# Tile 0's product in halves ahead of the leftovers, weights added on GpSimd; layer 1's direct sums scaled in pieces

## The chip, the cores and the metric

One core of one Trainium2 chip. The metric is the device time of one execution in microseconds (us). In what follows a run is one execution; each kernel was run several times, in rounds that alternate with the kernel before on the same chip. "The span" is the time from the first to the last instruction of the one execution that was traced; the run's time is about 1.7 us longer. In the profile lines PE is TensorE, PEld its weight loads, DVE VectorE, ACT ScalarE, POOL GpSimd and SP SyncE; L347 is line 347 of that run's kernel, and the numbers shift a little from kernel to kernel. A "hole" is a stretch in which TensorE is idle, a product's "lead" the time by which it is ready before TensorE wants it.

## The reference, cut to what matters

Two layers of a compressed interaction network on `x` of 4096 rows, 32 fields, 16 columns. Each layer multiplies every pair of fields elementwise, mixes the products with a weight matrix, and normalizes over the whole batch. Half of layer 1's outputs ("direct") go straight to the result, the other half feed layer 2.

```python
def _cin_layer(out, x, W, b, gamma, beta):
    h = jnp.einsum('rne,rfe->rnfe', out, x).reshape(r, -1, e)
    h = jnp.einsum('rce,oc->roe', h, W) + b[None, :, None]
    return _batchnorm(h, gamma, beta)            # mean and variance over rows and columns
h1 = _cin_layer(x, x, W1, b1, g1, beta1)         # 32x32 pairs -> 128
out, direct1 = (h1[:, :64], h1[:, 64:])
direct2 = _cin_layer(out, x, W2, b2, g2, beta2)  # 64x32 pairs -> 128
return jnp.concatenate([direct1, direct2], axis=1).sum(axis=-1)
```

## The kernel before

Layer 1 works through 128 tiles of 512 sites (a site is one row and column). As the pairs (i, j) and (j, i) have the same product, their weights are added (`w1 += w1m`) and only half of the products are made: per tile a "main" product of 128x2048 on VectorE, and per eight tiles one "leftovers" product of 128x512 for the 16 pairs (i, i+16). TensorE takes four main matmuls a tile, each 128x512, and per four tiles four small leftovers matmuls that open four accumulators. Each of these matmuls stands in the traces as two passes (1024 for the 512 main matmuls), so a tile's main matmuls are x8. The order in the code at the start is the leftovers' product, the main product, the leftovers' matmuls, the main matmuls; in the traces VectorE makes tile 0's main product first, then adds the weights, then makes the leftovers' product:

```python
BEGIN = 6                                        # warm-up matmuls on ones, ahead of everything
...
        nc.vector.tensor_tensor(w1_sb, w1_sb, w1m_sb, ALU.add)
...
        for t in range(NT):
            s = t % GROUP                        # GROUP = 8
            if s == 0:
                zr = rpool.tile([P, T], FP, tag="zr", name="zr")
                nc.vector.tensor_tensor(zr, r[:, :T], r[:, T:], ALU.mult)
            ...                                  # loads of tile t+1
            product = nc.vector.tensor_tensor(z, a..., b..., ALU.mult)     # 128x2048
            if s % 4 == 0:
                for k in range(4):
                    ps = pss[t + k] = psum.tile([P, T], FP, tag="ps", name="ps")
                    rows = slice(32 * k, 32 * (k + 1))
                    nc.tensor.matmul(ps, w1_sb[rows, 4 + s // 4, :], zr[rows, :], start=True, stop=False)
            for m in range(4):
                nc.tensor.matmul(pss[t], w1_sb[:, m, :], z[:, m // 2, m % 2, :], start=False, stop=(m == 3))
            if t > 0:
                finish(t - 1)                    # evict, statistics, sum of the direct half
            if t == 20:
                combine_weights()                # sums of layer 2's weights, six VectorE instructions
            with tc.issue_after(loads[-1].ins), tc.issue_after(product.ins):
                if t == 6:
                    nc.sync.dma_start(w2_sb, w2)
                for first, load in EARLY:        # layer 2's first loads, at t = 12 ... 112
                    if t == first:
                        early.append(load())
```

Layer 2 takes its 64 pairs of tiles in a Strassen-like scheme: ScalarE makes a factor into PSUM, VectorE multiplies it with loaded data (L456 and L461 of before), GpSimd sums these products (L502, L505), TensorE multiplies both kinds (L486). In the first pair of it the direct sums of layer 1 are finished and written:

```python
            if c == 0 and k == 1:
                with tc.issue_after(lasts["dve"].ins), tc.issue_after(lasts["act"].ins):
                    write_direct()     # a reduction, four tiny factors, one 128x2048 scaling, two writes on ScalarE's queue
```

## Time and profile before

| what | kernel before | read from |
|---|---|---|
| time | 2128.49 us, median of 3 (2127.01 to 2129.0) | the runs |
| span | 2125.7 us | the trace |
| TensorE busy | 2094.9 us | busy shares |
| leftovers' first matmul | 12.09 us | timeline |
| last statistics of layer 1 begin | 493.90 us | timeline of VectorE |
| from there to the end | 1631.8 us | 2125.7 less 493.90 |

The last two rows cut the program in two: whatever part 1 of the change does must show in the first number, whatever part 2 does in the second. One line marks the cut:

```profile
493.90 0.70 DVE L106 BATCH_NORM_STATS2 stats<-ps 128x6 f32<-128x512 f32 x1 [2.02 <-PE ps L357]
```

### The profile page before, as it was taken

How to read it: one execution, taken by the hardware profiler on the slowest of the kernel's cores; microseconds unless marked ns; L12 is line 12 of the kernel's file. 1: busy time of each engine (PE TensorE's matmuls, PEld its weight loads, DVE VectorE, ACT ScalarE, POOL GpSimd, SP SyncE). 2: the span in 40 equal slices, each digit the busy share in tenths (PEclk: the TensorE clock that was granted, in tenths of full speed). 3: DMA queues.
4: the chain of work that ended last, by engine and by line, in shares of the span. 5: the costliest groups of instructions: out<-in, count | busy, mean ns of one | idle time of the engine just before them, and what ended most of it. 6: DMA issues, size and time to landing. Idle time of an engine off the chain costs nothing.

```text
span 2125.7 us, 23431 instructions
## 1 busy us (share of the span) xinstructions
PE 2094.9 (99%) x8732; PEld 736.7 (35%) x8732; DVE 1912.0 (90%) x1461; ACT 855.6 (40%) x1233; POOL 1328.7 (63%) x390
## 2 busy tenths in 40 slices
PE   9999999999999999999999999999999999999996
PEld 3444444443333333333333333333333333333332
DVE  7988889887999999899999998999999989999996
ACT  3555555554333333333333333333333333433332
POOL 0000000003888888878888888788888888888885
PEclk9999999999999999999999999999999999999998
DMA  9999999998667777776768777776677777766751
GB/s 353 360 331 349 326 360 350 362 334 220 161 168 170 178 185 172 172 173 160 164 163 198 173 171 174 173 163 166 162 178 171 170 175 173 163 165 162 171 137 40
DMA packets 112019, 440.65 MB, mean 207 GB/s; under 512 B 13088, under 2 KB 13088, under 8 KB 103456
## 3 DMA queue, kind: packets, MB, share of 16 engines
q1 hardware_dynamic: 105296, 417.38, 73.4%
q10 hardware_dynamic: 6608, 21.77, 2.7%
q8 instruction: 68, 1.11, 0.2%
q14 instruction: 47, 0.39, 0.1%
HBM read 417.07 MB, written 22.02 MB: 207 GB/s over the span
## 4 chain that ended last, share of the span: by engine, by line
PE 85%; POOL 9%; DVE 3%; issue 2%; ACT 1%; DMA 0%; DVEq 0%; SPq 0%; POOLq 0%
PE x L486 62%; PE ps L357 21%; POOL t L505 5%; POOL t L502 3%; PE ps L355 2%; DVE zz L456 2%; ACT both L448 1%; DVE e L451 0%; DMA b<-in_xb 0%; DVE zz L461 0%; PE running L375 0%; DVE x L188 0%; DVE d L647 0%; ACT u L448 0%; DVE groupsx L124 0%
## 5 line engine op out<-in xcount | busy, mean ns | idle before, releaser
L486 PE MATMUL x<-zz,w_sb 128*64 128x512 f32 x2560 | 966.1, 592 | 0.0
L486 PE MATMUL x<-zz,s_sb 128*64 128x512 f32 x2048 | 932.4, 592 | 0.7 <-PE running L375 0.7
L502 POOL TENSOR_TENSOR t<-zz 128x1024 f32<-128x1024 f32 x192 | 456.9, 2380 | 760.4 <-DVE zz L456 760.4
L505 POOL TENSOR_TENSOR t<-zz,t 128x2048 f32<-128x2048 f32 x192 | 876.2, 4564 | 15.1
L486 PE MATMUL x<-t,s_sb 128*64 128x512 f32 x1536 | 696.2, 594 | 6.7 <-POOL t L505 6.7
L448 ACT ACTIVATE f<-a,keep 128x512 f32<-128x512 f32 x512 | 398.2, 778 | 632.7 <-DVE zz L456 626.7
L456 DVE TENSOR_TENSOR zz<-f,b 128x2048 f32<-128x2048 f32 x255 | 580.2, 2275 | 1.2 <-ACT f L448 1.2
L456 DVE TENSOR_TENSOR zz<-f,bx 128x2048 f32<-128x2048 f32 x255 | 580.2, 2275 | 0.0
L357 PE MATMUL ps<-z,w_sb 128*128 128x512 f32 x1024 | 449.2, 597 | 0.0
L486 PEld LDWEIGHTS x<-zz,s_sb 128*64 128x64 f32 x2048 | 280.5, 137 | 366.1 <-issue 350.3
L486 PEld LDWEIGHTS x<-t,s_sb 128*64 128x64 f32 x1536 | 205.3, 137 | 456.4 <-issue 397.3
L486 PE MATMUL x<-t,w_sb 128*64 128x512 f32 x768 | 363.1, 595 | 0.0
L345 DVE TENSOR_TENSOR z<-a,b 128x2048 f32<-128x2048 f32 x128 | 293.0, 2289 | 62.7 <-DMA b<-in_xb 33.3
L486 PEld LDWEIGHTS x<-zz,w_sb 128*64 128x64 f32 x2560 | 300.7, 137 | 109.6 <-issue 105.3
L357 PEld LDWEIGHTS ps<-z,w_sb 128*128 128x128 f32 x1024 | 192.4, 190 | 255.0 <-issue 244.7
L486 PE MATMUL x<-zz,neg_sb 128*64 128x512 f32 x512 | 240.6, 592 | 0.0
L307 ACT ACTIVATE e<-ps,bn_sb 128x512 f32<-128x512 f32 x127 | 87.3, 687 | 241.1 <-PE ps L357 235.7
L451 DVE TENSOR_TENSOR both<-both,x 128x512 f32<-128x512 f32 x64 | 44.0, 687 | 129.0 <-ACT both L448 129.0
L448 ACT ACTIVATE u<-e,bn_sb 64x512 f32<-64x512 f32 x64 | 46.2, 722 | 192.9 <-DVE e L451 192.9
L486 PEld LDWEIGHTS x<-zz,neg_sb 128*64 128x64 f32 x512 | 70.1, 137 | 145.9 <-issue 145.9
L486 PEld LDWEIGHTS x<-t,w_sb 128*64 128x64 f32 x768 | 100.1, 137 | 0.0
L448 ACT ACTIVATE both<-x 64x512 f32<-64x512 f32 x64 | 38.0, 593 | 137.5 <-PE x L486 137.5
(74 smaller groups left out, 892.3 us busy)
## 6 DMA issues: line engine op xcount, KB each, us to landing
a<-h SPq DMA_DIRECT2D x256, 512.0 KB, 5.4
a<-in_xa SPq DMA_DIRECT2D x128, 512.0 KB, 6.0
b<-in_xb SPq DMA_DIRECT2D x128, 512.0 KB, 7.0
b<-in_xb SPq DMA_DIRECT2D x64, 1024.0 KB, 7.2
bx<-in_xb SPq DMA_DIRECT2D x64, 512.0 KB, 6.2
bx<-x SPq DMA_DIRECT2D x64, 512.0 KB, 7.9
h<-kept ACTq DMA_DIRECT2D x64, 256.0 KB, 5.9
r<-in_xr SPq DMA_DIRECT2D x16, 512.0 KB, 8.0
```

The lines of the kernel that those rows point to most:

```text
L307: nc.scalar.activation(e, ps, AF.Identity, bias=b1)
L345: product = nc.vector.tensor_tensor(z, a.rearrange("p (a t) -> p a t", a=2).unsqueeze(2).to_broadcast([P, 2, 2, T]), b.rearrange("p (b t) ...
L355: nc.tensor.matmul(ps, w1_sb[rows, 4 + s // 4, :], zr[rows, :], start=True, stop=False)
L357: nc.tensor.matmul(pss[t], w1_sb[:, m, :], z[:, m // 2, m % 2, :], start=False, stop=(m == 3))
L448: return queue("act", lambda: nc.scalar.activation(to, source, AF.Identity, **scale_bias))
L451: return dve(lambda: nc.vector.tensor_tensor(to, x, y, ALU.add))
L456: dve(lambda: nc.vector.tensor_tensor(z, a, b.rearrange("p (k q) t -> p k q t", k=2), ALU.mult))
L486: queue("pe", lambda: nc.tensor.matmul(self.of[x], w, b, start=start, stop=stop))
L502: queue("pool", lambda: nc.gpsimd.tensor_tensor(t2, t3, b11, ALU.add))
L505: queue("pool", lambda: nc.gpsimd.tensor_tensor(t[:, 1:3], z[:, 2:4], twice, ALU.subtract))
```

## The change

Its intent is to let TensorE begin earlier, and to take work out of the first pair of layer 2. Part 1: tile 0's product is made in two halves, its main matmuls go first and the leftovers come behind; the weights are added on GpSimd; two reductions (`spread`, `block`) move from the start to tiles 12 and 14. Part 2: the direct sums' reduction moves to the second pair of layer 2, their factors to the third, the scaling is cut into four pieces over the pairs after it, and the writes go out in the ninth pair on SyncE's queue.

```diff
-    nc.vector.tensor_reduce(spread, select..., AX.X, ALU.max)      # and block
-        nc.vector.tensor_tensor(w1_sb, w1_sb, w1m_sb, ALU.add)
+        nc.gpsimd.tensor_tensor(w1_sb, w1_sb, w1m_sb, ALU.add)
...
-            if s == 0:
-                zr = ...                                            # leftovers first
+            if s == 0 and t > 0:
+                zr = leftovers(r)
+            for k in (slice(0, 1), slice(1, 2)) if t == 0 else (slice(0, 2),):
+                product = multiply_main(z, *main[0], k)
+            if t == 0:
+                with tc.issue_after(product.ins):
+                    zr = leftovers(r)
...
+            if s % 4 == 0 and t > 0:
+                add_leftovers(t, zr)
             for m in range(4):
-                nc.tensor.matmul(pss[t], ..., start=False, stop=(m == 3))
+                nc.tensor.matmul(pss[t], ..., start=(t == m == 0), stop=(t > 0 and m == 3))
+            if t == 0:
+                add_leftovers(t, zr)
...
+                if t == 12:
+                    nc.vector.tensor_reduce(spread, ...)
+                if t == 14:
+                    nc.vector.tensor_reduce(block, ...)
...
-    idle, swaps = [], []
+    idle, swaps = [lambda: sum_direct(NC - 1)], []
...
-            if c == 0 and k == 1:
-                with tc.issue_after(lasts["dve"].ins), tc.issue_after(lasts["act"].ins):
+            if c == k == 2:
+                queue("act", direct_factors)
+            if 3 <= c < 7 and k == 2:
+                queue("act", lambda: scale_direct(c - 3))           # 128x512 each
+            if c == 8 and k == 2:
+                with tc.issue_after(loads[-1].ins):
                     write_direct()                                  # now on nc.sync
```

More of the change, by code (lines that the diff above doesn't have):

```diff
@@ L230, in tile_cin @@
     spread = const.tile([KEEP, P], FP, tag="spread", name="spread")
-    nc.vector.tensor_reduce(spread, select.rearrange("k i n f -> k (n f) i"), AX.X, ALU.max)
     block = const.tile([KEEP, 4], FP, tag="block", name="block")
-    nc.vector.tensor_reduce(block, select.rearrange("k i n f -> k i (n f)"), AX.X, ALU.max)
     hs = [dram.tile([KEEP, 2 * T], FP, tag=f"h{c}", name=f"h{c}") for c in range(NC)]
@@ L324, in sum_direct @@
         def sum_direct(c):
-            nc.vector.tensor_reduce(
+            return nc.vector.tensor_reduce(
                 d1[:, c * RT : (c + 1) * RT],
@@ L330, in sum_direct, with leftovers, add_leftovers, multiply_main @@
             )
+        def leftovers(r):
+            zr = rpool.tile([P, T], FP, tag="zr", name="zr")
+            nc.vector.tensor_tensor(zr, r[:, :T], r[:, T:], ALU.mult)
+            return zr
+        def add_leftovers(t, zr):
+            for k in range(4):
+                rows = slice(32 * k, 32 * (k + 1))
+                ended = t == k == 0
+                nc.tensor.matmul(
+                    pss[t + k], w1_sb[rows, 4 + t % GROUP // 4, :], zr[rows, :], start=not ended, stop=ended
+                )
+        def multiply_main(z, a, b, k):
+            n = k.stop - k.start
+            return nc.vector.tensor_tensor(
+                z[:, k],
+                a.rearrange("p (a t) -> p a t", a=2)[:, k].unsqueeze(2).to_broadcast([P, n, 2, T]),
+                b.rearrange("p (b t) -> p b t", b=2).unsqueeze(1).to_broadcast([P, n, 2, T]),
+                ALU.mult,
+            )
         main = [load_main(0)]
@@ L335, in tile_cin @@
             s = t % GROUP
-            if s == 0:
-                zr = rpool.tile([P, T], FP, tag="zr", name="zr")
-                nc.vector.tensor_tensor(zr, r[:, :T], r[:, T:], ALU.mult)
             if s == 4 and t + 4 < NT:
@@ L342, in tile_cin @@
                 main.append(load_main(t + 1))
-            a, b = main.pop(0)
+            if s == 0 and t > 0:
+                zr = leftovers(r)
             z = zpool.tile([P, 2, 2, T], FP, tag="z", name="z")
-            product = nc.vector.tensor_tensor(
-                z,
-                a.rearrange("p (a t) -> p a t", a=2).unsqueeze(2).to_broadcast([P, 2, 2, T]),
-                b.rearrange("p (b t) -> p b t", b=2).unsqueeze(1).to_broadcast([P, 2, 2, T]),
-                ALU.mult,
-            )
+            for k in (slice(0, 1), slice(1, 2)) if t == 0 else (slice(0, 2),):
+                product = multiply_main(z, *main[0], k)
+            main.pop(0)
+            if t == 0:
+                with tc.issue_after(product.ins):
+                    zr = leftovers(r)
             if s % 4 == 0:
                 for k in range(4):
-                    ps = pss[t + k] = psum.tile([P, T], FP, tag="ps", name="ps")
-                    rows = slice(32 * k, 32 * (k + 1))
-                    nc.tensor.matmul(ps, w1_sb[rows, 4 + s // 4, :], zr[rows, :], start=True, stop=False)
+                    pss[t + k] = psum.tile([P, T], FP, tag="ps", name="ps")
+            if s % 4 == 0 and t > 0:
+                add_leftovers(t, zr)
             for m in range(4):
-                nc.tensor.matmul(pss[t], w1_sb[:, m, :], z[:, m // 2, m % 2, :], start=False, stop=(m == 3))
+                nc.tensor.matmul(
+                    pss[t], w1_sb[:, m, :], z[:, m // 2, m % 2, :], start=(t == m == 0), stop=(t > 0 and m == 3)
+                )
+            if t == 0:
+                add_leftovers(t, zr)
             if t > 0:
@@ L362, in tile_cin @@
             with tc.issue_after(loads[-1].ins), tc.issue_after(product.ins):
+                if t == 12:
+                    nc.vector.tensor_reduce(spread, select.rearrange("k i n f -> k (n f) i"), AX.X, ALU.max)
+                if t == 14:
+                    nc.vector.tensor_reduce(block, select.rearrange("k i n f -> k i (n f)"), AX.X, ALU.max)
                 if t == 6:
@@ L397, in tile_cin, with direct_factors @@
         evict_direct(eds[NC - 1][high, :], last)
-    def write_direct():
-        sum_direct(NC - 1)
-        direct = const.tile([P, 2], FP, tag="direct", name="direct")
+    direct = const.tile([P, 2], FP, tag="direct", name="direct")
+    def direct_factors():
         for half in range(2):
@@ L404, in write_direct, with scale_direct @@
                 to = direct[half * KEEP : (half + 1) * KEEP, k : k + 1]
-                nc.scalar.activation(to, ss1[high, k : k + 1], AF.Identity, scale=factor)
-        nc.scalar.activation(d1, d1, AF.Identity, scale=direct[:, 0:1], bias=direct[:, 1:2])
+                last = nc.scalar.activation(to, ss1[high, k : k + 1], AF.Identity, scale=factor)
+        return last
+    def scale_direct(part):
+        d = d1[:, part * T : (part + 1) * T]
+        return nc.scalar.activation(d, d, AF.Identity, scale=direct[:, 0:1], bias=direct[:, 1:2])
+    def write_direct():
         for half in range(2):
-            nc.scalar.dma_start(
+            nc.sync.dma_start(
                 out[:KEEP, half * (ROWS // 2) : (half + 1) * (ROWS // 2)],
```

## The prediction

> **What bounds the kernel now.** I read the page's busy shares first, then who waited for whom on TensorE, then the timeline of the start and of the opening of layer 2.
>
> ```profile
> PE 2094.9 (99%) x8732; PEld 736.7 (35%) x8732; DVE 1912.0 (90%) x1461; ACT 855.6 (40%) x1233; POOL 1328.7 (63%) x390
> ...
> PE x L486 <- POOL t L505: 6.7, 13, 2.4
> PE ps L355 <- DVE zr L338: 3.0, 1, 3.0
> PE begun L215 <- DVE ones L212: 1.6, 1, 1.6
> PE x L486 <- PE running L375: 0.7, 1, 0.7
> ```
>
> TensorE is busy for 2094.9 of 2125.7 us, and the change removes no matmul. Only TensorE's holes can be won, and they are listed: about 20 us behind its last matmul (untouched here), 3.0 us before the first leftovers (L355), 6.7 us in layer 2 behind GpSimd. There is no wait at all between 12 and 493.7 us.
>
> The start, in the timeline (start, duration, engine, line, what; in brackets the idle time before it):
>
> ```profile
> 8.27 2.29 DVE L345 TENSOR_TENSOR z<-a,b 128x2048 f32<-128x2048 f32 x1 [6.51 <-DMA b<-in_xb]
> 10.48 0.95 DVE L273 TENSOR_TENSOR w_sb<-w_sb,w1m_sb 128x768 f32<-128x768 f32 x1
> 11.35 0.68 DVE L338 TENSOR_TENSOR zr<-r 128x512 f32<-128x512 f32 x1
> 12.09 1.64 PE L355 MATMUL ps<-zr,w_sb 32*128 32x512 f32 x8 [3.04 <-DVE zr L338]
> ...
> 13.48 2.27 DVE L345 TENSOR_TENSOR z<-a,b 128x2048 f32<-128x2048 f32 x1
> ```
>
> Data of tile 0 is there at 8.2 us, then VectorE works three things off in a row before TensorE may begin: the whole product, the weights, the leftovers' product. The warm-up matmuls ended at 9.05 (12.09 less 3.04). The stretches by window show a second cost (columns: window, its length, busy time of PE, PEld, DVE, ACT, POOL, then the granted clock, DMA share, GB/s):
>
> ```profile
> 12.00:14.00 2.00, 1.91 (x9) 0.66 (x10) 2.00 (x4) 0.00 (x0) 0.00 (x0) 0.65 1.07 416
> 14.00:16.00 2.00, 2.00 (x3) 0.82 (x3) 1.94 (x3) 0.00 (x0) 0.00 (x0) 0.50 0.94 328
> 16.00:18.00 2.00, 2.00 (x6) 0.84 (x5) 2.00 (x1) 0.00 (x0) 0.00 (x0) 1.00 0.64 225
> ```
>
> After the hole the clock is halved until 16 us. The price is in the chain of waits, first group against second:
>
> ```profile
> 12.09 1.64 PE ps L355 x8
> 13.72 15.09 PE ps L357 x32
> 28.81 1.07 PE ps L355 x8
> 29.88 13.93 PE ps L357 x32
> ```
>
> The first eight leftover passes and 32 main passes last 16.72 us, start to start; the second set 15.00. So 1.72 us are lost to the clock.
>
> **What the Trainium skill says.** "TensorE: Matmul & The Clock Gate", Part 1: the half-rate state returns after an idle window of about 3.4 us, windows run freely, and full rate takes another such window of work. The trace agrees: idle 9.05 to 12.09, half rate from about 12.6 to 16.0. "VectorE: DVE Perf Modes", section on the TRN2 errata, gives (N+151)/0.96 ns for an fp32 tensor_tensor; the trace has 2.29 us for 2048 and, at L461, 1.21 to 1.23 us for 1024 elements. "GPSIMD Engine Reference", section 3.1, has an add of 2048 at 4497 ns, 1.96 times VectorE's; the trace has 4.57 us. "DMA: Bandwidth & Descriptors", "Issuing engines are not separate DMA queues": another issuing engine saves only issue time; before, ScalarE's queue spends 2.34 us issuing the two output writes.
>
> **The change part by part.**
>
> Part 1, the start. Tile 0's product becomes two products of 1024. The first starts at 8.27 as before and ends 1.23 later, at 9.50 (L461's duration); TensorE follows VectorE by 0.06 (12.03 to 12.09), so it starts at 9.56. The weights must be added by then. On GpSimd, 1024 elements take 2.38 us and 2048 take 4.57, so 768 interpolate to 1.83; the second weight load was issued at 1.32 and landed 5.1 us later, at 6.4; the add ends near 8.3. It is hidden, by 1.2 us. The order of instructions of the new kernel confirms that the first main matmuls wait for VectorE and GpSimd and stand ahead of the leftovers. The second half is done at about 10.6, before the first half's two matmuls (1.72 us of passes) end at 11.3. Leftovers: r landed at 9.5 (2.18+7.3), their product lies at 10.6 to 11.3 and is needed at 13.0. The hole falls from 3.04 to about 0.5 us, far below a window, so the clock should stay up. Won: 12.09-9.56 = 2.53, plus 1.72 of clock, 4.25 us in all.
>
> What takes some back at once: tile 1. Its b was issued at 3.40 and took 8.6 us: 12.0. In the kernel before VectorE came to it only at 13.48, so this was hidden. Now: 12.0+2.3 = 14.3 against TensorE ready at 9.56+3.43+1.07 = 14.06. Cost 0.3; 3.95 us are left.
>
> Then tiles 4 to 16. TensorE moves 3.95 us forward, the products less: loads of tile t+3 go out when product t ends, and those move by 13.48-12.0 = about 1.45. Between 16 and 22 us the DMA share is 0.64 to 0.87, so that fits in; from 22 us on it is 0.99 and more, so it cannot be much more. The products' lead over TensorE before was 4.3 us at tile 4 (ends 25.47, wanted 29.81), 3.6 at tile 8 (41.28 for 44.88), 2.8 at tile 11 (52.39 for 55.2), 3.3 at tile 14 (63.48 for 66.75) and 2.7 at tile 15 (67.47 for 70.2). It shrinks by 2.5: enough everywhere, though only 0.2 to 0.3 at tiles 11 and 15. But the two reductions taken from the start (1.02 and 0.67) come back here: the order of instructions puts one between products 12 and 13 and one between 14 and 15. The first falls into the 2.0 us that VectorE waited for b ahead of product 14. The second, some 0.6, makes product 15 about 0.5 late. Later the lead recovers: product 118 waits for b until 450.81 and still ends 3.7 us before it is wanted, and 50 products wait for TensorE, so the loads keep up. Cost about 0.5; 3.4 us are left.
>
> Part 2, the direct sums. Removed from the first pair of layer 2: a reduction of 0.67 on VectorE, four small and one 2.10 us activation, and 2.34 us of DMA issue on ScalarE, which made VectorE wait 1.18 us at 513.87. But TensorE's holes there come from GpSimd:
>
> ```profile
> 507.83 2.38 POOL L502 TENSOR_TENSOR t<-zz 128x1024 f32<-128x1024 f32 x1 [505.35 <-DVE zz L456]
> 510.29 4.53 POOL L505 TENSOR_TENSOR t<-zz,t 128x2048 f32<-128x2048 f32 x1
> 514.77 2.37 POOL L502 TENSOR_TENSOR t<-zz 128x1024 f32<-128x1024 f32 x1
> 517.23 4.56 POOL L505 TENSOR_TENSOR t<-zz,t 128x2048 f32<-128x2048 f32 x1
> 521.74 2.38 POOL L502 TENSOR_TENSOR t<-zz 128x1024 f32<-128x1024 f32 x1
> 524.19 4.54 POOL L505 TENSOR_TENSOR t<-zz,t 128x2048 f32<-128x2048 f32 x1
> ```
>
> GpSimd runs without a gap from 507.83, and starts after products that precede the removed work. The three holes behind it (2.36, 0.74, 0.72) stay: worth 0. The added work: the reduction now lies in the second pair, 0.6 us ahead of that pair's GpSimd work; GpSimd's last piece ended at 552.78 and was wanted at about 553.74, so 0.36 is left of 0.96. Four activations of about 0.7 (one eviction of 512 columns was 0.68) fall into ScalarE's gaps of 2.54 between factors. The writes move to SyncE's queue in the ninth pair, where the DMA share is about 0.70. Cost 0.
>
> Sum: 4.25-0.3-0.5 = 3.4 us; 2128.5-3.4 = 2125.1 us.
>
> **The rivals.** First, late products: if loads do not move forward at all after tile 3, tiles 4 to 15 lose another 1 to 1.4 us and the gain is about 2: 2126.4. For it: the DMA share of 0.99 from 22 us. Against it: the slack before, and the long-run lead. Second, the clock falls anyway, because windows run freely or the hole is longer than I think (GpSimd late, first loads late): a cold start costs 1.7, leaving about 1.7, 2126.8. Against it: a hole of 0.5 is a seventh of a window. Third, part 2 pays: the freed VectorE time of 1.85 us shortens the opening of layer 2, by at most the 3.8 us of its three holes: 2122 to 2124. Against it: GpSimd's unbroken run. Fourth, part 2 costs: layer 2 runs with hardly any spare time per pair (ten further waits for GpSimd of about 0.3 each exist already), so an activation or a write in the way of a factor may add 0.3 in each of seven pairs, 2 us: 2127.
>
> **Range and chances.** The runs before spread over 2 us, so the median is good to about 0.8. The start is worth 3 to 4 us with some certainty, the give-back 0 to 1.5, part 2 plus or minus 1. Predicted 2125.1 us, 8 in 10 between 2123.2 and 2127.0. A change of 2% would be 42 us, more than all the holes together: faster 0.003, within 2% 0.994, slower 0.003.
>
> **What would show it.** Right: first main matmul near 9.6 us, no half clock after it, tile 1 waiting about 0.3 us for its product; sub-microsecond waits for products at tiles 11 to 15; the end of layer 1 near 490.4 instead of 493.86; first piece on GpSimd 3.4 us earlier as well, and the same three holes behind it. Wrong: half clock after 9.6 us, a wait for GpSimd's weights, TensorE waiting in layer 1 for more than 1.5 us in sum, or a distance from the end of layer 1 to the end that differs by over 0.5 us from before.

## The result, and the profile after

The changed kernel took 2124.68 us (median of 4, 2124.06 to 2127.26) against 2128.3 (median of 4, 2127.01 to 2129.0) for the kernel before in the same rounds. The ratio is 0.9986, 95% interval 0.9969 to 1.0003: the same at 2%, and 3.6 us less by the medians. This interval still reaches past 1; those of after_again and start_only below do not. A ratio here is, to within 0.0001, the mean time of one kernel's runs over that of the other's of the same rounds, so it is not quite the ratio of the two medians. The predicted 2125.1 us lies 0.4 us off.

But the trace taken beside this result did not look like the prediction. It fell on the slowest of the four runs, 2127.26 us (span 2125.5). Its timeline of the start (start, duration, engine, line, what; idle time before it in brackets):

```profile
8.18 1.80 POOL L271 TENSOR_TENSOR w_sb<-w_sb,w1m_sb 128x768 f32<-128x768 f32 x1 [5.70 <-DMA w1m_sb<-in_w1m]
9.10 3.09 DVE L347 TENSOR_TENSOR z<-a,b 128x1024 f32<-128x1024 f32 x2 [7.34 <-DMA b<-in_xb]
11.21 5.37 PE L378 MATMUL ps<-z,w_sb 128*128 128x512 f32 x8 [2.23 <-DVE z L347]
16.50 1.14 PE L340 MATMUL ps<-zr,w_sb 32*128 32x512 f32 x8
```

and its stretches (the granted clock is the third number from the end):

```profile
12.00:14.00 2.00, 2.00 (x4) 0.86 (x3) 1.94 (x4) 0.00 (x0) 0.00 (x0) 0.61 0.98 381
14.00:16.00 2.00, 2.00 (x4) 0.67 (x2) 1.72 (x2) 0.00 (x0) 0.00 (x0) 0.53 0.98 373
```

Four things are off at once: the second weight load landed at 8.03 us instead of the 6.38 that the kernel before had, tile 0's data at 9.1 instead of 8.27, the two halves took 3.09 us rather than the 2.36 of two products of 1.23 us that overlap a little (after_third), and after a hole of 2.23 us the clock was halved all the same, so eight passes took 5.29 us, start to start. The last statistics of layer 1 then began at 493.71, hardly earlier than before. Is this how the changed kernel runs, or one unlucky execution? The first experiment asks that.

### The profile page after: what moved, and what is told of

Same layout as the page of the kernel before. It is cut to its first block, busy times and chain, and to the rows that moved or that the text cites. A ratio compares the mean times of both kernels' runs of the same rounds, so it can differ in the third digit from the quotient of the medians.

```text
span 2125.5 us, 23438 instructions
## 1 busy us (share of the span) xinstructions
PE 2095.5 (99%) x8732; PEld 736.3 (35%) x8732; DVE 1911.2 (90%) x1461; ACT 856.5 (40%) x1236; POOL 1330.4 (63%) x391
## 4 chain that ended last, share of the span: by engine, by line
PE 85%; POOL 9%; DVE 3%; issue 2%; ACT 1%; DMA 0%; DVEq 0%; SPq 0%; POOLq 0%
PE x L521 62%; PE ps L378 21%; POOL t L540 6%; POOL t L537 3%; PE ps L340 2%; DVE zz L491 2%; ACT both L483 1%; DMA b<-in_xb 0%; DVE e L486 0%; DVE zz L496 0%; PE running L404 0%; DVE x L188 0%; DVE z L347 0%; DVE d L687 0%; ACT u L483 0%
## 5 line engine op out<-in xcount | busy, mean ns | idle before, releaser
L347 DVE TENSOR_TENSOR z<-a,b 128x2048 f32<-128x2048 f32 (+1 forms) x129 | 293.6, 2277 | 62.8 <-DMA b<-in_xb 35.9
```

Source lines behind the costliest of these rows:

```text
L347: return nc.vector.tensor_tensor(z[:, k], a.rearrange("p (a t) -> p a t", a=2)[:, k].unsqueeze(2).to_broadcast([P, n, 2, T]), b.rearrange( ...
```

## The experiments

Twelve runs were made, in four sessions, each session on one chip. All outputs are right. Theory A is that of the prediction: the gain is the earlier start of TensorE and the clock that stays up; part 2 is worth nothing. Rivals: part 2 brings the gain (B); the clock alone does (C); and for what is lost on the way, GpSimd's addition or the moved reductions are to blame (D, E). The table holds the results; the readings follow.

| label | edit | median (range) of its runs | before, same rounds | ratio [95%] | first main matmul | last statistics of layer 1 | rest |
|---|---|---|---|---|---|---|---|
| after_again | none | 2124.74 (2123.97 to 2127.33) | 2129.12 | 0.9985 [0.9972, 0.9997] | 9.90 | 490.69 | 1631.9 |
| start_only | part 1 alone | 2124.65 (2124.01 to 2125.48) | 2129.12 | 0.9983 [0.9970, 0.9995] | 9.82 | 491.00 | 1631.9 |
| direct_only | part 2 alone | 2128.06 (2125.58 to 2130.38) | 2129.12 | 0.9997 [0.9985, 1.0010] | (leftovers 11.71) | 492.62 | 1631.9 |
| warm_before | before, three more warm-ups | 2127.66 (2127.42 to 2130.57) | 2129.12 | 1.0000 [0.9987, 1.0014] | (leftovers 12.54) | 493.94 | 1631.8 |
| gpsimd_beside | GpSimd work added | 2138.16 (one run) | 2128.89 | none | 9.88 | 504.16 | 1632.2 |
| dve_weights | weights on VectorE again | 2126.10 (2125.37 to 2127.30) | 2128.89 | 0.9987 [0.9975, 1.0000] | 9.27 | 492.56 | 1632.0 |
| late_reduce | reductions at tiles 60, 62 | 2124.78 (2124.05 to 2125.87) | 2128.89 | 0.9981 [0.9968, 0.9993] | 9.73 | 490.52 | 1632.6 |
| combined | both of these, one more warm-up | 2125.70 (2123.99 to 2128.87) | 2128.89 | 0.9986 [0.9972, 0.9999] | 9.46 | 491.74 | 1632.3 |
| after_third | none | 2124.72 (2124.09 to 2126.30) | 2127.47 | 0.9990 [0.9976, 1.0003] | 9.76 | 490.61 | 1631.7 |
| relaxed | late_reduce, layer 2's weights and loads spread | 2124.70 (2124.25 to 2124.97) | 2127.47 | 0.9987 [0.9975, 1.0000] | 9.97 | 490.79 | 1632.1 |
| relaxed_dve | combined, spread likewise | 2124.24 (2123.34 to 2126.76) | 2127.47 | 0.9987 [0.9975, 1.0000] | 10.43 | 493.15 | 1631.9 |
| before_again | kernel before, none | 2128.21 (2126.47 to 2132.77) | 2128.86 | 1.0006 [0.9993, 1.0020] | (leftovers 12.04) | 492.69 | 1632.0 |

Times in us. "Rest" is the span less the column ahead of it. Each timed kernel had five runs; the kernel before had nine in each of the four sessions, and five more as the control before_again, 41 in all.

### after_again: the changed kernel once more

No edit.

> The changed kernel unchanged, for a second trace, since the first trace fell on a run of 2127.26 us while the three others took 2124.1 to 2125.0. Theory (the start pays): an ordinary run is 3.5 to 4.2 us faster than before, b of tile 0 lands near 8.2 us, the first main matmul begins near 9.6 us, no half clock follows, and TensorE leaves layer 1 near 490.5 us. Rival (the start is always late and the gain comes from layer 2): the trace shows the start at 11 us and the half clock again, and layer 2 shorter by 2 us or more.

The median came back (2124.74), and the trace, now on a run of 2124.36 us, shows what the prediction had drawn:

```profile
6.87 1.80 POOL L271 TENSOR_TENSOR w_sb<-w_sb,w1m_sb 128x768 f32<-128x768 f32 x1 [4.39 <-DMA w1m_sb<-in_w1m]
8.29 2.60 DVE L347 TENSOR_TENSOR z<-a,b 128x1024 f32<-128x1024 f32 x2 [6.53 <-DMA b<-in_xb]
9.90 3.67 PE L378 MATMUL ps<-z,w_sb 128*128 128x512 f32 x8 [1.25 <-DVE z L347]
12.45 2.29 DVE L347 TENSOR_TENSOR z<-a,b 128x2048 f32<-128x2048 f32 x1 [0.78 <-DMA b<-in_xb]
13.50 1.14 PE L340 MATMUL ps<-zr,w_sb 32*128 32x512 f32 x8
14.80 6.71 PE L378 MATMUL ps<-z,w_sb 128*128 128x512 f32 x15 [0.16 <-DVE z L347]
```

```profile
12.00:14.00 2.00, 2.00 (x8) 0.69 (x10) 1.55 (x1) 0.00 (x0) 0.00 (x0) 1.00 1.05 420
14.00:16.00 2.00, 1.84 (x11) 0.68 (x4) 1.65 (x2) 1.33 (x3) 0.00 (x0) 1.00 0.98 381
```

The second fence has the stretches of the same trace. The hole is 1.25 us, the clock stays at 1.00, and the eight passes take 3.60 us where they took 5.29. TensorE waits once for tile 1's product, as foretold, and the last statistics of layer 1 begin at 490.69. So the first trace was one unlucky execution; but the spread between executions is itself part of the story, and after_third below was run to see it again.

### start_only and direct_only: which part brings it

start_only keeps the second half of the code as it was before; direct_only keeps the first half:

```diff
# start_only, against the changed kernel: part 2 undone
-    idle, swaps = [lambda: sum_direct(NC - 1)], []
+    idle, swaps = [], []
-            if c == k == 2: ... / if 3 <= c < 7 and k == 2: ... / if c == 8 and k == 2: ...
+            if c == 0 and k == 1:
+                write_direct()
# direct_only, against the kernel before: only these lines of the change
```

> Part 1 alone: tile 0 in halves, leftovers behind, weights added on GpSimd, the two reductions moved; the direct sums as before. Theory: all of the gain, 3.4 to 4.2 us below before. Rival (part 2 pays too): 1 to 2.5 us below before.

> Part 2 alone: the direct sums in pieces, the start as before. Theory: 0 within 0.4 us, the three waits of TensorE for GpSimd in the first pair stay at 2.4, 0.7 and 0.7 us. Rival (the freed VectorE and ScalarE time opens layer 2 sooner): 1 to 3 us faster.

start_only has all of the gain (ratio 0.9983), direct_only none (0.9997). The interval of direct_only would still allow 3 us, so the traces have to decide: its time after layer 1 is 1631.9 us, where the kernel before has 1631.8. B falls. Where the time of part 2 went shows in two views. The waits between 498 and 530 us, before the change and with part 2 alone:

```profile
PE x L486 <- POOL t L505: 3.8, 3, 2.4
```

```profile
PE x L492 <- POOL t L511: 3.8, 3, 2.4
```

Same sum, same number of waits, same longest one. And in the changed kernel's trace (after_again), GpSimd begins at 504.71 and works without a gap, while VectorE, rid of its reduction and of its wait for ScalarE, merely waits longer for TensorE's sums (5.20 us; in the kernel before it was 3.26):

```profile
504.71 2.37 POOL L537 TENSOR_TENSOR t<-zz 128x1024 f32<-128x1024 f32 x1 [496.04 <-DVE zz L491]
507.16 4.54 POOL L540 TENSOR_TENSOR t<-zz,t 128x2048 f32<-128x2048 f32 x1
511.65 2.39 POOL L537 TENSOR_TENSOR t<-zz 128x1024 f32<-128x1024 f32 x1
...
522.88 0.69 DVE L486 TENSOR_TENSOR both<-both,x 128x512 f32<-128x512 f32 x1 [5.20 <-ACT both L483]
```

The freed time became idle time of an engine that is not the bound there. Taking work off it could not help.

### warm_before: the clock alone

```diff
-BEGIN = 6
+BEGIN = 9
```

> The kernel before with nine warm-up matmuls in place of six, so that TensorE has work until about 11.6 us and the hole ahead of the first leftovers falls from 3.0 to about 0.5 us, with the first leftovers still at about 12.1. It tells the cost of the clock apart from the late start. Theory (the half clock costs 1.7 us of the start): 1.7 us faster, no half clock in the trace, first group of 40 passes 15.0 us long. Rival (the hole costs only its own length): no faster.

Three more warm-up matmuls keep TensorE busy until 12.60 us, 0.4 us past the leftovers' product, so the clock stayed up, and the second group of matmuls began at 27.54 instead of 28.74. Yet the ratio is 1.0000 (the median 1.5 us lower, the interval 3 us wide to either side), and the last statistics of layer 1 begin at 493.94. The 1.2 us were given back at two places: a wait of 0.34 us for the product at tile 7 and one of 0.29 at tile 15, and the two groups around them, leftovers included, took 15.60 and 15.64 us instead of 15.00. This was the first sign that in layer 1 the loads lead TensorE by little: whoever arrives earlier waits later. So in this trace a clock that stayed up won nothing. C alone does not explain the gain, though the interval here is too wide to settle the clock's worth; before_again below does.

### gpsimd_beside: does GpSimd's addition slow VectorE?

In the first trace the halves took 3.09 us. The Trainium skill, "SBUF — State Buffer", section "Who interferes with whom", says that a VectorE instruction with two inputs in SBUF contends with a GpSimd instruction that reads SBUF, not with one that only writes it. The experiment puts both beside layer 1's products (VectorE also sets the scratch tile to ones, once, at the start):

```diff
+            with tc.issue_after(product.ins):
+                if 28 <= t < 36:
+                    nc.gpsimd.tensor_tensor(scratch, w2_sb[...], w2_sb[...], ALU.mult)   # 128x1024, reads SBUF
+                if 44 <= t < 52:
+                    nc.gpsimd.memset(scratch, 1.0)                                       # only writes
```

> The changed kernel with eight GpSimd multiplications of 128x1024 (read and write on-chip memory) and then eight GpSimd memsets of 128x1024 (write only) put beside the products of layer 1, behind the landing of layer 2's weights near 36 us; the result is not changed. In the traces of the changed kernel the first half product took 1.55 and 1.96 us instead of 1.21 where the weights' addition on GpSimd still ran. Theory (a VectorE product with two on-chip operands stands still while a GpSimd instruction that reads runs, or the other way): beside the multiplications either products last 2.3 to 2.4 us longer than 2.29 or GpSimd's 2.38 us grow by as much; beside the memsets the products stay at 2.29. Rival (the first half was long for another reason, such as the loads landing): products stay at 2.29 throughout.

(The expectation's 1.55 us is a misreading: the first half product took 1.46 us in after_again, 1.64 in start_only and 1.96 in the first trace.) The eight multiplications all ran early, in one row from 33.8 us, and the memsets behind them:

```profile
33.77 26.45 POOL L391 TENSOR_TENSOR scratch<-w_sb 128x1024 f32<-128x1024 f32 x8 [25.25 <-DMA w_sb<-in_w]
39.36 4.43 DVE L347 TENSOR_TENSOR z<-a,b 128x2048 f32<-128x2048 f32 x1
50.84 4.43 DVE L347 TENSOR_TENSOR z<-a,b 128x2048 f32<-128x2048 f32 x1
...
60.29 8.02 POOL L398 MEMSET scratch<- 128x1024 f32 x8
60.43 2.28 DVE L347 TENSOR_TENSOR z<-a,b 128x2048 f32<-128x2048 f32 x1
63.24 2.27 DVE L347 TENSOR_TENSOR z<-a,b 128x2048 f32<-128x2048 f32 x1
```

The kernel's products take 2.29 us where GpSimd rests. A product beside a memset takes the same 2.28, one beside a multiplication of GpSimd up to 4.43, and GpSimd's own instructions take 3.31 us on average (26.45 by 8) where layer 2's additions of the same size take 2.38. (Those run beside products as well, but these have one input in PSUM, and they keep their 2.28 us.) The page is right in this case, in both directions. The kernel as a whole took 13 us longer than the changed kernel, nearly all of it in layer 1 (its last statistics begin at 504.16 us instead of 490.69).

With that, the start can be read exactly. In each trace with the addition on GpSimd:

| trace | addition ends | first half begins | they overlap by | first half lasts |
|---|---|---|---|---|
| relaxed (below) | 8.42 | 8.60 | none | 1.23 |
| late_reduce | 8.35 | 8.35 | 0.00 | 1.23 |
| gpsimd_beside | 8.52 | 8.51 | 0.01 | 1.23 |
| after_third | 8.53 | 8.38 | 0.15 | 1.23 |
| after_again | 8.67 | 8.29 | 0.38 | 1.46 |
| start_only | 8.59 | 8.03 | 0.56 | 1.64 |
| first trace | 9.98 | 9.10 | 0.88 | 1.96 |

From 0.15 us of overlap on, the half is longer by just the overlap less 0.15, and it ends 1.08 us after GpSimd in the last three cases: it stands still until GpSimd is done. D holds, though only for executions in which the second weight load is late against tile 0's data.

### dve_weights, late_reduce, combined: undo the two suspects

```diff
# dve_weights
-        nc.gpsimd.tensor_tensor(w1_sb, w1_sb, w1m_sb, ALU.add)
+        weights1 = nc.vector.tensor_tensor(w1_sb, w1_sb, w1m_sb, ALU.add)    # ahead of the first half
# late_reduce
-                if t == 12:    ...spread...     -                if t == 14:    ...block...
+                if t == 60:    ...spread...     +                if t == 62:    ...block...
# combined: both, and
-BEGIN = 6
+BEGIN = 7
```

> The changed kernel with the weights added on VectorE again, but ahead of tile 0's first half product, while VectorE waits for b. Theory (the addition on GpSimd costs the first half product 0.3 to 0.7 us): first half product 1.2 us, 0.3 us faster than the changed kernel in the trace's end of layer 1, more where loads land late; 3.6 to 4.5 us below before. Rival (the addition on VectorE costs as much, since the second weight load lands only shortly before b): same as the changed kernel.

> The changed kernel with the two reductions for layer 2 moved from tiles 12 and 14 to tiles 60 and 62, where the products' lead over TensorE has grown again. Theory (they make product 15 late): no time lost by TensorE in tiles 12 to 15, 0.2 to 0.4 us faster than the changed kernel at the end of layer 1. Rival (the loads of those tiles set it): the loss of 0.2 to 0.4 us in tiles 12 to 15 stays.

> Weights on VectorE ahead of the first half product, the two reductions at tiles 60 and 62, and seven warm-up matmuls in place of six, so that the hole ahead of the first main matmul is nearly closed also where loads land late. Theory: no half clock, 0.4 to 0.8 us faster than the changed kernel, 4 to 5 us below before, with a smaller spread from run to run. Rival: as fast as the changed kernel, because what is won at the start is lost at tiles 9 to 16 to late products, as in the run with warm-up matmuls alone.

dve_weights does what it was made for. The addition takes 0.96 us on VectorE and fits ahead of tile 0's data; the halves take 2.36, and TensorE begins 1.28 us after the first half does (after_again: 1.61):

```profile
6.72 0.96 DVE L271 TENSOR_TENSOR w_sb<-w_sb,w1m_sb 128x768 f32<-128x768 f32 x1 [4.95 <-DMA w1m_sb<-in_w1m]
7.99 2.36 DVE L347 TENSOR_TENSOR z<-a,b 128x1024 f32<-128x1024 f32 x2 [0.31 <-DMA b<-in_xb]
9.27 3.70 PE L379 MATMUL ps<-z,w_sb 128*128 128x512 f32 x8 [0.77 <-DVE z L347]
...
14.58 1.98 PE L379 MATMUL ps<-z,w_sb 128*128 128x512 f32 x4 [0.54 <-DVE z L347]
```

And it is no faster for it: 2126.10 us. It lost 0.54 us at tile 1 at once, and a further 0.77 at tiles 12 to 15, 0.55 between 281 and 296 us, 1.01 between 311 and 327. late_reduce still loses 0.34 us at tiles 12 to 15, though there is no reduction any more: product 15 ends at 66.68 us, against 66.85 and 66.70 in after_again and after_third. So E falls. combined loses 1.49 us in 310 to 326 us, where the first pair's data of layer 2 are being loaded (1 MB at tile 80) on top of layer 1's own loads:

```profile
311.19 7.13 PE L379 MATMUL ps<-z,w_sb 128*128 128x512 f32 x16
318.76 3.70 PE L379 MATMUL ps<-z,w_sb 128*128 128x512 f32 x8 [0.43 <-DVE z L347]
322.98 3.70 PE L379 MATMUL ps<-z,w_sb 128*128 128x512 f32 x8 [0.53 <-DVE z L347]
```

A new theory, F, follows: layer 1 has pinch points, at the places where layer 2's weights and first data are loaded beside layer 1's, and a lead that TensorE gains at the start is partly eaten there.

### after_third, relaxed, relaxed_dve: is it those loads?

after_third is the changed kernel a third time. relaxed is late_reduce with the pinch points spread out; relaxed_dve is combined with the same spreading:

```diff
-                if t == 6:
+                if t == 24:
                     nc.sync.dma_start(w2_sb, w2)
-            if t == 20:
-                combine_weights()
+            if t in range(44, 56, 2):
+                with tc.issue_after(product.ins):
+                    combine_weights((t - 44) // 2)               # one of its six instructions each
-    EARLY += [(72, lambda: load_b(0)), (80, lambda: load_bx(0))]
+    EARLY += [(72, lambda: load_b(0)), (80, lambda: load_bx(0)), (84, lambda: load_bx_rest(0, early[-1]))]
```

> The changed kernel once more, as the measure for the two runs beside it on the same chip: 2124.1 to 2125.3 us in most runs.

> The changed kernel with what loads VectorE and the load queue in layer 1 spread out: layer 2's weights loaded at tile 24 in place of 6 and combined one piece at a time at tiles 44 to 54, the two reductions at tiles 60 and 62, the second half of the first bx load at tile 84 in place of 80. Theory (between tile 2 and the end of layer 1 TensorE loses time only where extra loads or extra VectorE work meet a thin lead): no loss after tile 1 in the trace, end of layer 1 at about 490.3 us, 0.2 to 0.4 us faster than the changed kernel. Rival (the loads of layer 1 by themselves are too slow for a TensorE that started earlier): losses of the same size at tiles 4 to 16 or later.

> The same spreading, with the weights on VectorE ahead of the first half product and seven warm-up matmuls, as in the combined kernel. Theory: what the combined kernel lost at tiles 80 to 84 (1.5 us in its trace) is gone, end of layer 1 at about 490.0 us, 1 to 1.5 us faster than the combined kernel, 4.5 to 5 us below before, the fastest of all. Rival: as slow as the combined kernel, 3 us below before.

At the first pinch point F holds. The same group of 32 passes (tiles 12 to 15) in late_reduce and in relaxed, where 14.00 us is the time without a wait:

```profile
56.10 14.33 PE L378 MATMUL ps<-z,w_sb 128*128 128x512 f32 x32
```

```profile
56.71 14.00 PE L383 MATMUL ps<-z,w_sb 128*128 128x512 f32 x32
```

TensorE comes 0.61 us later here, and that alone would have covered the 0.34. But VectorE also makes product 15 1.34 us earlier, again late_reduce and then relaxed:

```profile
64.40 2.28 DVE L347 TENSOR_TENSOR z<-a,b 128x2048 f32<-128x2048 f32 x1
```

```profile
63.06 2.28 DVE L352 TENSOR_TENSOR z<-a,b 128x2048 f32<-128x2048 f32 x1
```

Its lead is 1.76 us, where in late_reduce it was 0.06. So the spreading did it, not the later start; which of its pieces did, was not separated.

relaxed does not wait anywhere in layer 1 after tile 1. But its first data came late (TensorE began at 9.97), so it arrives at the end of layer 1 with all the others, at 490.79. Its median, 2124.70, is that of the changed kernel; its five runs lie within 0.7 us, which may be chance. In relaxed_dve the losses only moved on, to 326 to 388 us, beside the further loads of layer 2 that begin at tile 88:

```profile
380.97 7.13 PE L384 MATMUL ps<-z,w_sb 128*128 128x512 f32 x16 [0.83 <-DVE z L352]
```

So F is shown for the place that was relieved, and is likely, not shown, for the later ones. No version here beats the changed kernel: relaxed_dve's median is 0.5 us below after_third's, its interval nearly the same.

### before_again: the kernel before, once more

No edit; a control.

> The kernel before, unchanged, for a second trace: its runs spread from 2125.3 to 2131.9 us, and the trace of part 2 alone, whose start is the same, had warm-up matmuls until 10 us and no half clock. Theory (how long the warm-up runs slowly, and whether the clock is halved after the hole, differ from run to run with the moment at which the clock's window falls): the ratio of times is 1.000; either trace pattern may appear, and the end of layer 1 in the trace goes with it, 493.9 us with the half clock and near 492.6 without. Rival (always as in the first trace): half clock from 12.6 to 16.0 us again.

It shows what the "clock" term was worth. Its leftovers begin at 12.04 us, where the first trace of before had 12.09, but this time the clock held:

```profile
12.04 1.14 PE L355 MATMUL ps<-zr,w_sb 32*128 32x512 f32 x8 [2.35 <-DVE zr L338]
```

```profile
12.00:14.00 2.00, 1.97 (x10) 0.80 (x11) 2.00 (x3) 0.00 (x0) 0.00 (x0) 1.00 1.07 379
```

A hole of 2.35 us, no half clock; the same was seen in direct_only (hole 1.66). And the last statistics begin at 492.69, so between the two executions of the kernel before lie 1.21 us, not 1.72: the faster one then lost 0.50 at tiles 12 to 15, where the slower one had waited for nothing. The half clock is an accident of part of the executions, not a property of the kernel before.

## Why the prediction was right, and where its terms were off

The total was right (2125.1 against 2124.68, and 2124.74 and 2124.72 in the repeats), and so was its mechanism: part 1 alone reproduces the gain, the rest after layer 1 takes 1631.7 to 1632.0 us in all traces of before, changed, start_only and direct_only alike. Term by term:

**First main matmul at 9.56, a gain of 2.53.** Measured 9.90 and 9.76 in the repeats, 11.21 in the unlucky trace; against 12.04 to 12.09 that is 2.1 to 2.3. What failed is the step "It is hidden, by 1.2 us". The addition was in time for TensorE, but it lay beside VectorE's first half, which reads two inputs from SBUF, and stopped it: by 0.24 us in after_again, 0.73 in the first trace. The prediction asked when GpSimd would be done, and not what it would do to its neighbour meanwhile. A further 0.1 us is that TensorE follows the half by 0.15 us here, not by 0.06 as in dve_weights and in before; why, the runs do not say.

**"Plus 1.72 of clock".** Right for the trace it was read from, wrong as a property. The measured value between the two executions of the kernel before is 1.21 us net, and only where the clock fell. Nor was "far below a window, so the clock should stay up" sure: it stayed up in the repeats (holes of 1.25 and 0.69 us), but fell in the first trace after 2.23. The prediction took the trace of before to agree with the idle window of about 3.4 us that it cites, though the idle time there, 9.05 to 12.09, was only 3.04 us. Its second rival, in its words "first loads late", is what that trace shows: its layer 1 ended 0.2 us ahead of before's.

**"Cost 0.3" at tile 1.** Measured 0.23 in after_again, from where the leftovers' eight passes of 1.07 us would have ended (13.50 + 1.07 = 14.57) to 14.80; 0.31 in after_third; none in start_only, whose loads were earlier. Right as a difference; both of its ends, the product and TensorE, came about 0.5 us later than foretold (14.75 for 14.3, 14.57 for 14.06).

**"Cost about 0.5" at tiles 12 to 15.** Measured 0.23 in after_again (14.23 us where 14.00 is due), 0.14 in after_third. Half the size, and the cause given, the moved reductions, was wrong: late_reduce loses 0.34 without them. relaxed, which moved the load of layer 2's weights and the sums of them as well, loses nothing. The step that failed is that the products move forward by "about 1.45": product 15 ended at 66.85 us in after_again and at 67.47 before, only 0.62 earlier, while TensorE came to it 3.3 us earlier (66.90 and 70.22). That used up the whole lead of 2.7 us; without the reductions (late_reduce) the product ended only 0.17 us earlier still. The prediction overlooked what stands just ahead of these tiles: the load of layer 2's weights (1 MB, issued at tile 6), and the six VectorE instructions that combine them, which the code names at tile 20 but the traces have between 35 and 51 us, with tiles 12 to 15 behind them from 55 us on. Which of the two holds the products back was not separated.

**Part 2, "Cost 0", and its gain of 0.** Right: direct_only's rest is 1631.9 us, before's 1631.8. The rival that part 2 pays and the one that it costs both fall by the waits quoted above.

**The sum.** The trace of before that the prediction used had the half clock, and from it to after_again the end of layer 1 moved by 3.21 us (493.90 to 490.69), for a predicted 3.4. Compared like with like, both with the clock up, it is 492.69 to 490.61 or 490.69, 2.0 to 2.1 us. So it is in part luck that the median came within 0.4 us of the prediction: 1.72 us of the sum were counted on in every execution, and are due in some only. The medians differ by 3.6, 4.4 and 2.8 us in the three sessions in which the changed kernel ran. Part of this, then, is an effect on the mixture: 13 of the changed kernel's 14 runs have a mean granted clock of 0.996 or better, but 19 of 41 runs of the kernel before have 0.994 or 0.995. These 19 average 2129.6 us, the 15 at 0.996 2128.1, the 7 at 0.997 2125.9. None of those slowest runs was traced, so where their clock was lost is open.

That the clock also falls elsewhere can be seen. At the opening of layer 2 TensorE waits some 2.4 us for GpSimd's first sum, in all 14 traces alike; in 6 of them (dve_weights, late_reduce, combined, relaxed, relaxed_dve, gpsimd_beside) half clock followed, in 8 it did not. The stretch behind the hole in late_reduce (hole 2.43 us, ended at 511.57) and in after_third (2.42 us, ended at 511.65):

```profile
513.00:517.00 4.00, 4.00 (x16) 1.18 (x14) 4.00 (x3) 1.56 (x2) 3.92 (x2) 0.79 1.02 223
```

```profile
513.00:517.00 4.00, 4.00 (x22) 1.42 (x20) 4.00 (x3) 1.56 (x2) 3.92 (x2) 1.00 0.99 215
```

The same hole within 0.01 us, at the same place, once with the clock at 0.79 and once at 1.00. It cost little there: the slower passes ate into the later waits for GpSimd (2.6 us in two waits instead of 3.9 in three), and the rest after layer 1 was 1631.9 to 1632.6 us in these six traces, 1631.7 to 1632.0 in the other eight. A hole of this length makes the half clock possible; the start holes of 0.42 to 1.66 us, in eight traces, were never followed by it.

Which execution it strikes can be worked out from the clock changes that each trace records. Within one trace they lie whole multiples of 3.413 us apart, from the warm-up to the end (before: 12.60 to 2111.80 us, 615 steps). So a grid of 3.413 us runs through each execution, and it lies differently in each; the Trainium skill, "TensorE: Matmul & The Clock Gate", Part 1, has such a window that runs on its own, and these traces agree. The holes, laid on the grid of their own trace:

| trace and place | hole | most of it in one step | half clock from |
|---|---|---|---|
| first trace, start | 2.23 | 2.16 | 12.46 |
| before, start | 3.04 | 2.90 | 12.60 |
| before_again, start | 2.35 | 1.57 | none |
| late_reduce, layer 2 | 2.43 | 2.13 | 511.27 |
| dve_weights, layer 2 | 2.36 | 2.07 | 513.25 |
| warm_before, layer 2 | 2.35 | 2.00 | none |
| after_third, layer 2 | 2.42 | 1.74 | none |

In all ten falls ahead of the program's end, TensorE had been idle for 2.07 us or more within one step, and the clock fell at the end of that step; the ten holes of 2.35 to 2.65 us without a fall had at most 2.00 us in any one step. (The ends of matmuls are modelled in a trace, so the border is not sharp.) The unlucky first trace had nearly all of its hole in one step.

## What to carry to other kernels

Work moved to an idle engine is free only if it does not stop a neighbour: before moving an elementwise operation to GpSimd, look at what VectorE does at that time and where its inputs lie. Before counting a saved wait as a gain, look for the next thing that the earlier arrival will have to wait for; here a lead of 2 us was all that the loads of layer 1 would carry, and every further 0.3 to 0.5 us at the start came back as waits later. And take more than one trace of a kernel before reading a term of a microsecond from it, since one execution's half clock is not the kernel's.

## What the Trainium skill lacked or had wrong

- "TensorE: Matmul & The Clock Gate", Part 1, gives an idle window of about 3.4 us for the fall to half rate. Here the grid agrees (3.413 us), but a step need not be idle throughout: 2.07 us of idleness in it sufficed (dve_weights), 2.00 did not (warm_before). For a hole, in these 14 traces: up to 1.7 us it was safe; of the 20 between 2.2 and 3.8 us ten were followed by half clock, as they lay to the grid.
- "SBUF — State Buffer", "Who interferes with whom": agreed with these runs, and the block is a full one (the half product ended 1.08 us after GpSimd in each of three traces). What it lacks is a size for alternating streams: products of 2.28 us took up to 4.43, GpSimd's instructions 3.31 on average where 2.38 is their time alone.
- No page found has the spread from one execution to the next of when the first loads land. Tile 0's product could begin anywhere from 7.89 to 9.15 us, and the second weight load landed between 6.38 and 8.16.
